# Shared tiles for the last keys of a cross-attention, and a key bias that rides as one more column

## The chip, the cores and the metric

The kernel runs on one core of one Trainium2 chip. The time is the device time of one execution in microseconds (us). Three executions of the kernel before took 1998.29, 2001.81 and 2000.94 us; their median is 2000.94. One more execution was profiled.

The engines are named as in the profile: PE (TensorE's matmuls), PEld (its weight loads), DVE (VectorE), ACT (ScalarE), POOL (GpSimd), SP (the queue that issues the DMAs).

## The reference, cut to what matters

Eight batches of 64 tokens go through one block of three parts: cross-attention over a context of 1601 tokens together with a self-attention, a sparse attention, and a feed-forward network with ternary weights. The change touches the cross-attention:

```python
# x: (8, 64, 512), cond = ctx_2048: (8, 1601, 512); 16 heads of 128, 8 groups of keys
qx = _fp8_linear_pertensor(ln_out, wqx, wqx_scale, qx_in_scale).reshape(b, s, g, hpg, d)
qx = _ln(qx, qxln_w, qxln_b)
kvx = jnp.einsum('bsi,oi->bso', cond, w_kv_x)
kx, vx = jnp.split(kvx, 2, axis=-1)
kx = _ln(kx.reshape(b, sc, g, d), kxln_w, kxln_b)      # weight and bias per key element
vx = vx.reshape(b, sc, g, d)
xout = _gqa(qx, kx, vx).reshape(b, s, nh * d)          # softmax(q k / sqrt(128)) v
```

A key is a normalised vector times `kxln_w` plus `kxln_b`. The bias adds the same number to all scores of one query row.

## The kernel before, in words

The 8 groups of keys are worked in two halves of 4 (`HG = 4`). One `Cross(b, half)` object does one batch for one half; there are 16 of them, half 0 first, batches 0 to 7 in each. The 1601 context tokens are cut into 13 tiles of 128 (`TT`); the last has 65 (1601 = 12 x 128 + 65). Six chunks of two tiles, the last of three (128 + 128 + 65 = 321), share a tile of keys and one of scores.

A hand-written loop over `g` (16 x 13 steps and a run-out of 20, 228 in all) sets the order of tracing. In step `g` it calls, each for another tile:

- `keys(tt)`: load a transposed context tile `cTr`, split it into a rounded high part (`cThi`, ACT) and the rest (`cTlo`, POOL), and form the key products on PE: three combinations of high and low parts by four pieces of the 512 inputs, twelve matmuls of 512 columns (L542). Then square and copy on ACT (L547, L548), sum on DVE (L549), the inverse root on POOL (L550, L173), and the scaling on DVE (L552). The mean is already taken out of the weights.
- `keys_t(tt)`, one step later: four transposes on PE (L219), then the scaled and biased key as high part `kthi` (ACT, L565), the scaled rest `kf` (DVE, L567), and the low part `ktlo`, which is `kf` plus the bias (ACT, L568).
- `scores(ci)` when a chunk is whole: three matmuls for each group (L587) and one DVE pass that moves the scores from PSUM and takes their row maximum (L591). The odd width 321 is filled up to 322 by zeroed key columns (POOL).
- `maxima`, `exps`, `probs_t`, `context`, `weigh` and `values`, some 13 to 17 steps later (`LAG = 17`): exponentials (L601), turned probabilities (L613), and their product with the context tile (L673 to L678), which is loaded again as `cr`.

All other work is written as generators in three streams, pumped at the end of every step: `bgA` (projections, self-attention and the tail of every token block) at `PACE[0]` yields a step until `g = LATER`, then `PACE[1]`; `bgB` (ternary weights) and `bgC` (the last token blocks). At step 135 the loop empties `bgA` in one go, before the batch halves of half 1 are concatenated.

A scheduler then draws up a fixed order for each engine: it takes what is ready in its own timeline, by priority, which is the order of tracing unless the code shifts it. `issue_after(pin[0].ins)` keeps background work on DVE behind the scaling of the newest keys. PSUM has 8 banks: 3 (`pm`) are shared by scores, keys, turned probabilities and values once the first steps are over, 1 is for the background, 4 hold the context sums.

Of the kernel before, what the change touches and what calls it, by code (L numbers as in the profile page):

```python
# [11 lines left out]
F32 = mybir.dt.float32  # L12
# [24 lines left out]
KTW = 324  # L37
NCH = len(CHUNKS)
CHUNK_OF = {tt: ci for ci, ch in enumerate(CHUNKS) for tt in ch}
LAG = 17  # L40
# [4 lines left out]
FAR = 3  # L45
PACE = 1.55, 4
LATER = 142
TERNARY_PACE, TERNARY_AT = 0.4, 8
# [9 lines left out]
def tile_perceiver(ctx: ExitStack, tc: tile.TileContext, t: dict):  # L58
# [432 lines left out]
    def key_weights(half):  # L491
# [11 lines left out]
        return hi, lo  # L503

    paced = [None]
    pin = [None]

    class Cross:


        def __init__(self, b, half):
            self.b, self.half = b, half
            self.raw = None
            self.S = {}
            self.kt = {}
            self.kn = {}
            self.pp = {}
            self.cc = {}
            self.mx = sm("cmx", HG * NCH, bufs=2)
            self.su = sm("csu", HG * NCH, bufs=2)  # L520

# [7 lines left out]
        def keys(self, tt):  # L529

            t0, n = TT[tt]
            raw = mp.tile([P, NIC, P], F32, tag="raw", name=nm("cTr"), bufs=3)
            paced[0] = nc.sync.dma_start(raw[:, :, :n], t["ctxT"][self.b].rearrange("(c p) k -> p c k", p=P)[:, :, t0:t0 + n])
            chi = mp.tile([P, NIC, P], F32R, tag="cThi", name=nm("cThi"), bufs=2)
            clo = mp.tile([P, NIC, P], F32R, tag="cTlo", name=nm("cTlo"), bufs=2)
            A.copy(chi[:, :, :n], raw[:, :, :n])  # L536
            GP.tensor_tensor(clo[:, :, :n], raw[:, :, :n], chi[:, :, :n].bitcast(F32), ALU.subtract)  # L537
            ps = kxp()
            k = 0
            for st, mv in ((chi, self.wk[0]), (chi, self.wk[1]), (clo, self.wk[0])):  # L540
                for ic in range(NIC):
                    PE.matmul(ps[:n], lhsT=st[:, ic, :n], rhs=mv[:, ic, :], start=k == 0, stop=k == 11)  # L542
                    k += 1
            kn = mp.tile([P, 512], F32, tag="kn", name=nm("kn"), bufs=3)
            sq = mp.tile([P, 512], F32, tag="sq", name=nm("sq"), bufs=1)
            v = sm("kxv", HG)
            A.activation(sq[:n], ps[:n], AF.Square, scale=1.0 / math.sqrt(D))  # L547
            A.copy(kn[:n], ps[:n])  # L548
            V.tensor_reduce(v[:n], v3(sq[:n], HG), AX.X, ALU.add)  # L549
            GP.tensor_scalar(v[:n], v[:n], EPS, None, ALU.add)  # L550
            r = rsqrt(v[:n], n, HG, "rqk")
            pin[0] = V.tensor_tensor(v3(kn[:n], HG), v3(kn[:n], HG), r.unsqueeze(2).to_broadcast([n, HG, D]), ALU.mult)  # L552
            self.kn[tt] = kn

        def keys_t(self, tt):

            t0, n = TT[tt]
            ci = CHUNK_OF[tt]
            c0 = TT[CHUNKS[ci][0]][0]
            if ci not in self.kt:  # L560
                self.kt[ci] = [mp.tile([P, HG, KTW], F32R, tag="kt" + x, name=nm("kt" + x), bufs=2) for x in ("hi", "lo")]
            hi, lo = self.kt[ci]
            pt = transpose4(self.kn.pop(tt), n, kxp())
            o = slice(t0 - c0, t0 - c0 + n)
            A.activation(hi[:, :, o], v3(pt, HG)[:, :, :n], AF.Identity, bias=hb["kx"], scale=hw["kx"])  # L565
            kf = mp.tile([P, HG, P], F32, tag="kf", name=nm("kf"), bufs=2)
            V.scalar_tensor_tensor(kf[:, :, :n], v3(pt, HG)[:, :, :n], hw["kx"], hi[:, :, o].bitcast(F32), ALU.mult, ALU.subtract)  # L567
            A.activation(lo[:, :, o], kf[:, :, :n], AF.Identity, bias=hb["kx"])  # L568

        def scores(self, ci):  # L570
# [3 lines left out]
            N = cw + (cw & 1)  # L574
            if N > cw:
                GP.memset(hi[:, :, cw:N].bitcast(F32), 0.0)
                GP.memset(lo[:, :, cw:N].bitcast(F32), 0.0)
            sc = mp.tile([P, HG, KTW], F32, tag="S", name=nm("S"), bufs=7)
            self.S[ci] = sc
            per = 512 // N  # L580
            for g0 in range(0, HG, per):
# [7 lines left out]
                for i, g in enumerate(gs):  # L589
                    ps = bank[:, i * N:(i + 1) * N]  # L590
                    V.tensor_tensor_reduce(sc[:, g, :cw], ps[:, :cw], zeros.to_broadcast([P, cw]), 1.0, -3.0e38,  # L591
                                           ALU.add, ALU.max, self.mx[:, g * NCH + ci:g * NCH + ci + 1])

        def maxima(self):
            self.nmx = sm("cnm", HG)
            V.tensor_reduce(self.nmx, v3(self.mx, HG), AX.X, ALU.max, negate=True)  # L596

# [371 lines left out]

    def gp_copy(dst, src):  # L970
        GP.tensor_scalar(dst, src, 1.0, 1.0, ALU.mult, ALU.mult)  # L971

    WIDEN = gp_copy, A.copy
# [155 lines left out]

    NT = len(TT)  # L1130
    work = [Cross(b, half) for half in range(2) for b in range(NB)]
# [10 lines left out]
    for g in range(NA + LAG + 3):  # L1142
# [27 lines left out]
        if g == 0:  # L1170
            bgA.pump(ALL)
        if g == 2:
            bgA.add(norms(rest), projection("qx", range(4), rest), projection("qx", range(4, 8), range(NJ)),
# [51 lines left out]
        for bg, q in ((bgA, PACE[g >= LATER]), (bgC, PACE[1]), (bgB, TERNARY_PACE if g < NA + FFN_AT else 0)):  # L1225
            n = int((g + 1) * q) - int(g * q)

            with tc.issue_after(pin[0].ins), tc.issue_after(paced[0].ins) if bg is bgB else nullcontext():
                bg.pump(n)
# [79 lines left out]
```

## Time and profile before

| | |
|---|---|
| median of three executions | 2000.94 us |
| the profiled execution | 1998.47 us |
| its span, first to last instruction | 1996.7 us |
| mean granted PE clock | 0.987 |
| PE matmuls | 10709, busy 1931.5 us |
| L542, twelve key products for each of 208 tiles | 832 + 832 + 832 matmuls |
| L568, low part of the keys on ACT | 208, busy 147.4 us |
| DMA, hardware queue | 349.97 MB, 55.8% of 16 engines |

In a row of grouped instructions the first number after the bar is the busy time of the group and the second the mean duration of one in ns; matmuls overlap, so durations of PE add up to more than the time they take. In a timeline row stand start, length, engine, line, what is written from what, shapes and a count. In a row of waits stand the total in us, how often, and the longest.

### The profile page before, as it was taken

What the parts mean: (1) busy time and instruction counts of PE and PEld (TensorE: products, weight loads), DVE (VectorE), ACT (ScalarE), POOL (GpSimd) and SP (SyncE); (2) the same over time, 40 slices, a digit from 0 to 9 for tenths busy, and PEclk for the clock granted to TensorE, in tenths of its full rate; (3) what the DMA queues carried; (4) which work ended last, traced back from release to release, by engine and by line L of the source; (5) the groups of instructions that cost most, each with busy time, mean ns of one, the idle gap of its engine ahead of it and who ended that gap; (6) DMA issues with size and microseconds to landing.
All of it is one profiled execution on the core that took longest, in us unless ns stands there. A gap on an engine that the chain in (4) does not pass through costs nothing. (4 is left out here: it accounts for less than half of the span.)

```text
span 1996.7 us, 32526 instructions
## 1 busy us (share of the span) xinstructions
PE 1931.5 (97%) x10709; PEld 1594.1 (80%) x10709; DVE 1357.9 (68%) x3324; ACT 1345.9 (67%) x2932; POOL 682.7 (34%) x807
## 2 busy tenths in 40 slices
PE   6899999999999999999999999999999999999998
PEld 5688887888888888888888888888877777886776
DVE  6868678667778677766775765666577665665665
ACT  6777777677778667765765655665786676676554
POOL 5443434333334434323233323323333323320132
PEclk9999999999999999999999999999999999999989
DMA  6354445466455654556886667656744633564415
GB/s 195 112 151 148 148 146 153 132 193 213 152 150 172 194 179 140 173 180 224 282 268 192 214 225 264 203 185 214 258 133 154 212 110 97 165 205 139 149 56 172
DMA packets 296507, 352.05 MB, mean 176 GB/s; under 512 B 30337, under 2 KB 191233, under 8 KB 296337
## 3 DMA queue, kind: packets, MB, share of 16 engines
q1 hardware_dynamic: 296336, 349.97, 55.8%
q8 instruction: 84, 1.38, 0.3%
q14 instruction: 87, 0.70, 0.1%
HBM read 283.94 MB, written 65.68 MB: 175 GB/s over the span
## 5 line engine op out<-in xcount | busy, mean ns | idle before, releaser
L537 POOL TENSOR_TENSOR cTlo<-cTr,cThi 128x512 fp32r<-128x512 f32 (+1 forms) x208 | 271.1, 1303 | 840.7 <-PE kx L542 443.8
L677 PE MATMUL acc<-plo,chi 128*128 128x512 f32 x768 | 311.7, 406 | 1.0 <-DVE plo L624 1.0
L678 PE MATMUL acc<-phi,clo 128*128 128x512 f32 x768 | 303.4, 396 | 0.0
L549 DVE TENSOR_REDUCE kxv<-sq 128x4 f32<-128x512 f32 (+1 forms) x208 | 141.9, 682 | 228.0 <-ACT sq L547 227.7
L542 PE MATMUL kx<-wkhi,cThi 128*128 128x512 f32 (+1 forms) x832 | 244.3, 415 | 6.6 <-DVE cmx L591 2.5
L676 PE MATMUL acc<-phi,chi 128*128 128x512 f32 x768 | 237.8, 403 | 4.6 <-ACT chi L653 3.4
L565 ACT ACTIVATE kthi<-kx,cols 128x512 fp32r<-128x512 f32 (+1 forms) x208 | 159.5, 767 | 106.8 <-PE kx L219 105.1
L542 PE MATMUL kx<-wklo,cThi 128*128 128x512 f32 (+1 forms) x832 | 231.0, 398 | 0.0
L542 PE MATMUL kx<-wkhi,cTlo 128*128 128x512 f32 (+1 forms) x832 | 226.3, 393 | 0.0
L173 POOL TENSOR_TENSOR rqk<-kxv,mhalf 128x4 f32<-128x4 f32 (+1 forms) x208 | 219.9, 1057 | 16.6
L653 ACT CAST chi<-cr 128x512 fp32r<-128x512 f32 x192 | 118.9, 619 | 137.7 <-PE acc L677 126.2
L536 ACT CAST cThi<-cTr 128x512 fp32r<-128x512 f32 (+1 forms) x208 | 125.6, 605 | 120.0 <-PE kx L542 48.4
L601 ACT ACTIVATE S<-S,cnm 128x256 f32<-128x256 f32 (+1 forms) x384 | 196.8, 520 | 1.5 <-DVE cnm L596 1.5
L567 DVE SCALAR_TENSOR_TENSOR kf<-kx,cols,kthi 128x512 f32<-128x512 f32 (+1 forms) x208 | 151.1, 726 | 60.0 <-ACT kthi L565 58.8
L542 PEld LDWEIGHTS kx<-wklo,cThi 128*128 128x128 f32 (+1 forms) x832 | 156.2, 188 | 39.7
L542 PEld LDWEIGHTS kx<-wkhi,cTlo 128*128 128x128 f32 (+1 forms) x832 | 153.5, 185 | 39.3 <-issue 0.8
L552 DVE TENSOR_TENSOR kn<-kn,rqk 128x512 f32<-128x512 f32 (+1 forms) x208 | 144.7, 695 | 57.0 <-POOL rqk L173 55.5
L542 PEld LDWEIGHTS kx<-wkhi,cThi 128*128 128x128 f32 (+1 forms) x832 | 147.2, 189 | 40.8 <-DVE cmx L591 5.0
L591 DVE CUSTOM_DVE_ANT_0 S<-s,zeros 128x256 f32<-128x256 f32 (+1 forms) x384 | 149.7, 429 | 43.8 <-PE s L587 43.5
L568 ACT ACTIVATE ktlo<-kf,cols 128x512 fp32r<-128x512 f32 (+1 forms) x208 | 147.4, 709 | 29.0 <-DVE kf L567 28.5
L676 PEld LDWEIGHTS acc<-phi,chi 128*128 128x128 f32 x768 | 139.0, 189 | 34.9 <-ACT chi L653 4.6
L677 PEld LDWEIGHTS acc<-plo,chi 128*128 128x128 f32 x768 | 145.2, 189 | 25.7 <-DVE plo L624 1.5
(339 smaller groups left out, 3938.3 us busy)
## 6 DMA issues: line engine op xcount, KB each, us to landing
cTr<-in_ctxT SPq DMA_DIRECT2D x192, 256.0 KB
cr<-in_ctx SPq DMA_DIRECT2D x192, 256.0 KB
ws<-wpd SPq DMA_DIRECT2D x88, 512.0 KB
clod<-clo SPq DMA_DIRECT2D x96, 256.0 KB
clo<-clod SPq DMA_DIRECT2D x96, 256.0 KB
wv<-in_wkv SPq DMA_DIRECT2D x64, 256.0 KB
tern<-in_ffn_w SPq DMA_DIRECT2D x64, 256.0 KB
wpd<-ws SPq DMA_DIRECT2D x32, 512.0 KB
```

The source lines that it names most:

```text
L173: GP.tensor_tensor(y[:n], v, mhalf[:n, :k], ALU.pow)
L537: GP.tensor_tensor(clo[:, :, :n], raw[:, :, :n], chi[:, :, :n].bitcast(F32), ALU.subtract)
L542: PE.matmul(ps[:n], lhsT=st[:, ic, :n], rhs=mv[:, ic, :], start=k == 0, stop=k == 11)
L552: pin[0] = V.tensor_tensor(v3(kn[:n], HG), v3(kn[:n], HG), r.unsqueeze(2).to_broadcast([n, HG, D]), ALU.mult)
L565: A.activation(hi[:, :, o], v3(pt, HG)[:, :, :n], AF.Identity, bias=hb["kx"], scale=hw["kx"])
L567: V.scalar_tensor_tensor(kf[:, :, :n], v3(pt, HG)[:, :, :n], hw["kx"], hi[:, :, o].bitcast(F32), ALU.mult, ALU.subtract)
L568: A.activation(lo[:, :, o], kf[:, :, :n], AF.Identity, bias=hb["kx"])
L591: V.tensor_tensor_reduce(sc[:, g, :cw], ps[:, :cw], zeros.to_broadcast([P, cw]), 1.0, -3.0e38, ALU.add, ALU.max, self.mx[:, g * NCH + ci:g ...
L601: A.activation(self.S[ci][:, g, :cw], self.S[ci][:, g, :cw], AF.Exp, bias=self.nmx[:, g:g + 1], accum_out=self.su[:, g * NCH + ci:g * NCH ...
L676: PE.matmul(self.U[ic], lhsT=chi[:n, s], rhs=phi[:n], start=tt == 0, stop=False)
L677: PE.matmul(self.U[ic], lhsT=chi[:n, s], rhs=plo[:n], start=False, stop=False)
L678: PE.matmul(self.U[ic], lhsT=clo[:n, s], rhs=phi[:n], start=False, stop=False)
```

## The change

Four things change.

1. **The 64 tokens before the odd one.** Tile 12 (tokens 1536 to 1599) of batches 2k and 2k+1 is loaded into one tile of 128 rows when the even batch comes to it, and one set of twelve products gives the keys of both. The odd batch's `keys(12)` returns at once; its rows wait in the tile `kn2` until its own `keys_t(12)`. The first two batches of half 0 are left unpaired (`UNPAIRED = 2`) and keep their tile of 65.
2. **The odd token.** `odd_keys` forms, once for each half (at `g = 30` and `g = 110`), the keys of token 1600 of all eight batches in one tile of eight rows. Each paired batch copies its column from there into its chunk (ACT).
3. **The keys' bias.** Keys are only scaled now: high part by ACT (`turned`), low part by DVE straight into `ktlo`. The bias becomes a key of its own, in the column that was zero before (column 322 of the last chunk). Its score, one number for each query row, is copied out of PSUM for each group (`qb`), and `maxima` adds it to the largest score and forms `qb - (top + qb)` as the exponent's offset.
4. **Order and memory.** `PACE` goes from 1.55 to 1.57, `LATER` from 142 to 145, pumped background work is traced under `tc.high_priority(-100)`, so 100 places later in priority, and the scratch for software DMA descriptors shrinks to 1024 bytes of a partition.

```diff
+NT = len(TT)
+ODD_AT = 30, 110
+UNPAIRED = 2
-PACE = 1.55, 4
-LATER = 142
+PACE = 1.57, 4
+LATER = 145
...
+    def turned(kn, n, parts, r0=0):
+        hi, lo = parts
+        pt = kxp()
+        for g in range(HG):
+            PE.transpose(pt[:, g * P:g * P + n], kn[:, g * P:(g + 1) * P], ident[r0:r0 + n, r0:r0 + n])
+        src = v3(pt, HG)[:, :, :n]
+        A.activation(hi, src, AF.Copy, scale=hw["kx"])
+        V.scalar_tensor_tensor(lo, src, hw["kx"], hi.bitcast(F32), ALU.mult, ALU.subtract)
+
+    def odd_keys(half):
+        raw = load(mp.tile([P, 512], F32, tag="raw", name=nm("oc"), bufs=3)[:NB], t["ctx"][:, SC - 1, :])
+        pt = kxp()
+        for ic in range(NIC):
+            PE.transpose(pt[:, ic * NB:(ic + 1) * NB], raw[:, ic * P:(ic + 1) * P], ident[:NB, :NB])
...
+        A.copy(chi[:, :, :NB], src)
+        V.tensor_tensor(clo[:, :, :NB], src, chi[:, :, :NB].bitcast(F32), ALU.subtract)
+        kn = normed_keys(wk[half], chi, clo, NB)
+        oddk[half] = [const.tile([P, HG, NB, 2], F32R, tag=f"odd{x}", name=nm("odd")) for x in ("h", "l")]
+        for x, y in zip(oddk[half], kb2):
+            gp_copy(x[:, :, :, 1], y.bitcast(F32).unsqueeze(2).to_broadcast([P, HG, NB]))
+        turned(kn[:NB], NB, [x[:, :, :, 0] for x in oddk[half]])
...
+    V.tensor_copy(kb, hb["kx"].to_broadcast([P, HG]))
+    V.tensor_copy(kb2[0], kb)
+    V.tensor_tensor(kb2[1], kb, kb2[0].bitcast(F32), ALU.subtract)
...
         def keys(self, tt):
             t0, n = TT[tt]
+            pair = tt == NT - 1 and self.paired
+            if pair and self.b % 2:
+                return
...
+            if pair:
+                n = P
+            for bi in range(2 if pair else 1):
+                w = S if pair else n
+                paced[0] = nc.sync.dma_start(raw[:, :, bi * S:bi * S + w], t["ctxT"][self.b + bi].rearrange("(c p) k -> p c k", p=P)[:, :, t0:t0 + w])
...
+            self.kn[tt] = normed_keys(self.wk, chi, clo, n, pair)
+            if pair:
+                work[self.half * NB + self.b + 1].kn[tt] = self.kn[tt]
...
         def keys_t(self, tt):
-            pt = transpose4(self.kn.pop(tt), n, kxp())
-            o = slice(t0 - c0, t0 - c0 + n)
-            A.activation(hi[:, :, o], v3(pt, HG)[:, :, :n], AF.Identity, bias=hb["kx"], scale=hw["kx"])
-            kf = mp.tile([P, HG, P], F32, tag="kf", name=nm("kf"), bufs=2)
-            V.scalar_tensor_tensor(kf[:, :, :n], v3(pt, HG)[:, :, :n], hw["kx"], hi[:, :, o].bitcast(F32), ALU.mult, ALU.subtract)
-            A.activation(lo[:, :, o], kf[:, :, :n], AF.Identity, bias=hb["kx"])
+            o = t0 - c0
+            kn = self.kn.pop(tt)
+            if tt < NT - 1 or not self.paired:
+                turned(kn[:n], n, [x[:, :, o:o + n] for x in self.kt[ci]])
+                if n & 1:
+                    for x, y in zip(self.kt[ci], kb2):
+                        gp_copy(x[:, :, o + n:o + n + 1], y.bitcast(F32).unsqueeze(2))
+                return
+            r = self.b % 2 * S
+            turned(kn[r:r + S], S, [x[:, :, o:o + S] for x in self.kt[ci]], r)
+            for x, y in zip(self.kt[ci], oddk[self.half]):
+                A.copy(x[:, :, o + S:o + S + 2], y[:, :, self.b, :])
...
         def scores(self, ci):
-            if N > cw:
-                GP.memset(hi[:, :, cw:N].bitcast(F32), 0.0)
-                GP.memset(lo[:, :, cw:N].bitcast(F32), 0.0)
...
+                    if N > cw:
+                        V.tensor_copy(self.qb[:, g:g + 1], ps[:, cw:N])
 
         def maxima(self):
+            top = sm("ctop", HG)
+            V.tensor_reduce(top, v3(self.mx, HG), AX.X, ALU.max)
+            V.tensor_tensor(top, top, self.qb, ALU.add)
             self.nmx = sm("cnm", HG)
-            V.tensor_reduce(self.nmx, v3(self.mx, HG), AX.X, ALU.max, negate=True)
+            V.tensor_tensor(self.nmx, self.qb, top, ALU.subtract)
...
+        if g in ODD_AT:
+            odd_keys(work[nA].half)
...
-            with tc.issue_after(pin[0].ins), tc.issue_after(paced[0].ins) if bg is bgB else nullcontext():
+            with tc.issue_after(pin[0].ins), tc.issue_after(paced[0].ins) if bg is bgB else nullcontext(), tc.high_priority( -100):
                 bg.pump(n)
...
-    nc = _bacc.Bacc("TRN2", target_bir_lowering=False, num_devices=1)
+    nc = _bacc.Bacc("TRN2", target_bir_lowering=False, num_devices=1, dynamic_dma_scratch_size=1024)
```

`normed_keys` is the second part of the old `keys` (products, squares, norm and scaling) as a function of its own; for a paired tile it writes to `kn2`, of which there is one, instead of `kn`, of which there are three.

## The prediction

> **What bounds the kernel now.** I read the page's first two parts, then the waits of TensorE (PE), then a timeline of single tiles, since busy time does not give the price of one matmul.
>
> ```profile
> span 1996.7 us, 32526 instructions
> PE 1931.5 (97%) x10709; PEld 1594.1 (80%) x10709; DVE 1357.9 (68%) x3324; ACT 1345.9 (67%) x2932; POOL 682.7 (34%) x807
> PE   6899999999999999999999999999999999999998
> PEclk9999999999999999999999999999999999999989
> ```
>
> PE is busy in every slice but the first two and the last; no other engine passes 68%, and the granted clock is full. So 1996.7 - 1931.5 = 65 us of the span are PE idle. The waits of PE say where, longest first:
>
> ```profile
> PE tr L219 <- DVE fa L201: 11.7, 2, 10.6
> PE pj L340 <- ACT ws L325: 5.0, 1, 5.0
> ...
> PE pt L613 <- DVE cmx L591: 3.9, 5, 1.4
> ...
> PE acc L676 <- ACT chi L653: 3.4, 2, 2.8
> PE kx L219 <- DVE kn L552: 3.0, 2, 1.9
> PE tr L372 <- ACT fb L385: 2.9, 1, 2.9
> PE pt L613 <- ACT S L601: 2.8, 2, 2.6
> PE kx L542 <- DVE cmx L591: 2.5, 6, 0.6
> PE pp L431 <- DMA ws<-wpd: 2.5, 3, 1.3
> ```
>
> The columns are total us, times, longest. Nothing repeats in every tile: 208 key tiles and 208 context tiles go by with some dozens of waits. Between the start and the last 150 us the kernel lasts as long as PE's instructions do. What one tile costs is read from starts, not from durations (here PE's timeline around one full tile, one 65-token tile, and the transposes of a 65-token tile):
>
> ```profile
> 707.95 1.09 PE L542 MATMUL kx<-wkhi,cThi 128*128 128x512 f32 x4
> 708.88 1.07 PE L542 MATMUL kx<-wklo,cThi 128*128 128x512 f32 x4
> 709.78 1.07 PE L542 MATMUL kx<-wkhi,cTlo 128*128 128x512 f32 x4
> ...
> 758.02 1.18 PE L542 MATMUL kx<-wkhi,cThi 128*65 128x512 f32 x4
> 759.03 1.10 PE L542 MATMUL kx<-wklo,cThi 128*65 128x512 f32 x4
> 759.97 1.10 PE L542 MATMUL kx<-wkhi,cTlo 128*65 128x512 f32 x4
> 760.91 0.60 PE L219 MATMUL kx<-ident,kn 128*128 128x128 f32 x4
> ...
> 768.69 0.41 PE L219 MATMUL kx<-ident,kn 65*128 65x65 f32 x4
> 768.93 0.61 PE L613 MATMUL pt<-ident,S 128*128 128x128 f32 x4
> ```
>
> A 65-token tile's twelve products run from 758.02 to 760.91, 2.89 us; a full one's first eight from 707.95 to 709.78, 1.83 us, so 2.75 for twelve. Sixty-five tokens cost what 128 cost. I use 2.8 us a tile, 0.234 a matmul. A small transpose is (768.93 - 768.69)/4 = 0.06 us.
>
> **The change part by part, TensorE.** Pairing starts at batch 2 in half 0 and at batch 0 in half 1: 3 + 4 = 7 pairs, so 7 of 208 key tiles disappear: 7 x 2.8 = 19.6 us less. The transposes stay, four a tile and batch (64 columns for 65). `odd_keys` runs twice; its eight tokens still move 512 columns in each of twelve products: 2 x 2.8 = 5.6 us more, and 16 small transposes at 0.06 are 1.0. The scores keep their 322 columns: the last, once zero, now holds the bias key. PE's work: -19.6 + 5.6 + 1.0 = **-13.0 us**.
>
> Two other prices were possible. By the page's mean (406 to 415 ns a matmul) 84 fewer and 24 more would be worth 60 x 0.41 = 25 us. Durations overlap: four of 0.4 us start within 0.93. And the Trainium skill ("TensorE: Matmul & The Clock Gate", section "Back-to-back issue gap") puts a sustained 512-column matmul in a real kernel at about 131 ns; by that the removed tiles save 11.0 us, the added cost 3.1, and PE gains only 7 us. The starts above say 0.225 to 0.24, so the measured number decides and I keep 13.0.
>
> **ScalarE (ACT).** The low part of the keys is now the subtraction itself, so L568 goes: 208 x 0.709 = 147 us. Five fewer tiles net (7 gone, 2 small come) take 5 x (0.59 + 0.58) = 6 of squares and copies. The odd columns add 28 copies at about 0.2 (nearest row: the 128x4 copy L633, 199 ns median), 5.6 us. ACT ends near 1346 - 147 = 1199 us, perhaps 19 less if the high part without bias is 0.09 shorter (L346, a scaled copy of 128x512 from PSUM, is 687 ns; L565 782). ACT is not the bound, so only PE waits that end in ACT can shrink. The rows above plus smaller ones make about 17 us, 2.2 of them the first weights, untouched. Gain between 0 and 13; with a tenth of ACT's work gone I take a third of 13: **-4 us**. What is late next in those waits is PE's own earlier work or DVE.
>
> **VectorE (DVE).** L567 writes the low part instead of `kf`, at the same 0.73. New in the last chunk are 4 copies of one PSUM column for each of 16 batch-halves: 64. No row of that shape; nearest is L817, a 64x8 copy from PSUM, 164 ns median: 10.5 us of DVE, covered on DVE itself at 68%. But each holds a score bank that long; before, a bank was held for 486 + 83 ns. PE now loses 3.9 + 2.5 = 6.4 us to L591. Bounds: 0 if another bank is free, 10.5 if every copy shows. A hold longer by 164/569, 29%, of waits of 6.4 gives **+2 us**. The two additional operations in `maxima` (about 0.17 each, as L596) delay the first exponentials by 0.35 us; probabilities are turned two loop steps later, some 17 us, which hides them; without that cover, 16 x 0.35 = 5.6. Three operations for `kb` at the start: at most 0.6, I take 0.3 into rounding.
>
> **GpSimd and the queues.** POOL loses 32 memsets of 0.103 and 5 x 1.3 of norms; it gains 4 + 4 small copies near 0.26. It is 34% busy: nothing. SP issues the same 208 key loads (each pair's tile takes two) plus two small ones, 0.38 us each, and the loads queued behind them are prefetched. `odd_keys` has a chain (load, transpose, copy, product, norm, transpose). PE's order is fixed at build, so a link that comes late holds everything behind it on PE. Bounds: 0, and 2 x 3 us by the longest PE waits on ACT and DVE in the middle (2.6 to 2.9): **+2 us**. `kn2` lives 13 loop steps, and the next pair wants it after 26; it holds nobody. In the odd batch's empty step PE moves 2.8 us earlier to the next tile, whose load may show; PE has no wait at all on `cTr` now, and ACT waits 16.0 us in total for it, so nothing taken.
>
> **Order and pace.** Background work (projections, self-attention, the tail of each token block) gets 100 places less priority; a loop step has 32526/228, about 143, instructions, so it yields by two thirds of a step. PE now waits on background tiles (pj, tr of L372, pp) 5.0 + 2.9 + 2.5 = 10.4 us; yielding gives their producers more time. No row prices a reordering: bounds -10 and +10 (it can create as many such waits), I take a fifth of what is to be had, **-2 us**. Pace 1.57 brings 3 steps ahead by loop step 135, where all the remaining background is issued at once (I count about 227 steps in all, so some 18 remain instead of 21). Between there and step 148 that queue is empty, so moving the switch from 142 to 145 changes nothing. The smaller scratch moves no data in this kernel: the page shows the hardware queue and instruction queues only. Nothing.
>
> Sum: -13.0 - 4 + 2 + 2 - 2 = **-15 us**. The profiled execution took 1998.47 (its span and 1.8 around it), so 1983.5 there. That execution lies 2.5 under the median of the runs, 2000.94; on the median the forecast is **1986 us**.
>
> **The rivals.**
> - More than the sum. ACT's relief and the new order remove half of the 65 us of idle PE time that is not start or tail (about 30 us): -13 - 15 = -28 or so, 1972. For it: many waits end in ACT or on background tiles. Against: some are PSUM banks waiting for DVE, which is not relieved. Chance 0.15.
> - Background deferred too far (the slower one). Its place is the producers of background tiles: weight splits on ACT and DVE (L325, L327), norms through POOL (44 `rq` powers of about 1.07 us). Placed behind the foreground, they end after PE's fixed order has arrived at their consumer. Price: one such wait for each of 227 background steps. It decides from 15/227 = 0.066 us a step; at 0.13 it costs 30, net +15, 2016. For it: the one 5.0 us wait of pj on ws shows how a late split hits PE. Against: only a handful of such waits now, with DVE and ACT a third idle. Chance 0.14, weighed at 2003 to 2020.
> - Banks. Every one of 64 column copies delays PE by its time and a signal, 0.25 us: 16 us instead of 2, net -1, 2000. Against: L591 shows in 11 PE waits while 384 banks pass. Chance 0.04.
> - PE's work falls but something else sets the pace, so nothing is seen: 1999 to 2002. Against: 97%. Chance 0.05.
>
> **How the numbers follow.** Main case 0.62, own range 1977 to 1996. Differences under 0.2%, 4 us, can hardly be told from none here: the three runs of before span 1998.29 to 2001.81. Faster by more than that: 0.62 + 0.15 = 0.77. Same: banks and nothing, 0.04 + 0.05, less a little given to slower: 0.08. Slower: 0.15. The range takes the main case, most of the larger gain and the no-change cases, with one tenth below and one above: 1968 to 2003.
>
> **What would show it.** PE's busy time near 1912 to 1920 with about 10665 matmuls, and L542's successor with 12 x 203 of them; ACT near 1180 to 1200 with no `ktlo` row on ACT; PE's idle between 58 and 66 us. The waits on `cmx` should be near 8 us, no more than 15. Wrong if PE's busy time falls by 13 and idle rises as much (the order), if new rows of pj, tr or pp waiting stand at the top of PE's waits, or if a transpose of `odd_keys` waits many us. A fall of the idle below 45 us is the larger gain.

## The result, and the profile after

The changed kernel took 2008.07 us (median of 8 executions, 2003.40 to 2014.02) beside 2001.01 us of the kernel before (8 executions, 1995.88 to 2003.34). The ratio is 1.0040, interval 1.0025 to 1.0055: slower by about 7 us, where 1986 us was forecast and 2003 was the upper end of the range. Each run below had the kernel before beside it on its chip, with medians of 1999.55 to 2001.45 us; two runs are best compared by their ratios to it.

From the page of the profile after, the span and the busy times:

```profile
span 2003.2 us, 32385 instructions
PE 1924.9 (96%) x10665; PEld 1593.9 (80%) x10665; DVE 1376.2 (69%) x3417; ACT 1206.4 (60%) x2739; POOL 673.6 (34%) x766
```

PE has 44 matmuls fewer and is busy 6.6 us less; ACT lost 139.5 us. But PE's idle is now 2003.2 - 1924.9 = 78.3 us, against 65.2 before. The work went down as meant, and the idle time rose by twice as much. The waits of PE (total us, times, longest) show where part of it shows up:

```profile
PE tr L222 <- DVE fa L204: 11.8, 3, 10.1
PE tr L375 <- ACT fa L370: 5.6, 4, 2.7
PE pj L343 <- ACT ws L328: 5.0, 1, 5.0
...
PE pt L676 <- DVE cqb L651: 4.0, 1, 4.0
...
PE po L488 <- ACT fb L480: 2.8, 1, 2.8
```

The two longest of before are still there, nearly unchanged (11.7 and 5.0 us). One row is new near the top, the `tr` transposes of background work that wait for `fa` of ACT (5.6 us in four waits). The bank waits have not grown in sum: those on `cmx`, 6.4 us before, are 1.9 in all, and the new copies `cqb` add 4.0 in a single wait. No one row carries what the change costs. So I used another reading. For every matmul I take the time to the next one's start. The median of that for its shape, over all the traces here (capped at 0.231 us for 512 columns), is its *work*; whatever a matmul takes beyond it is *stall*, which holds waits and slow clock alike. Before: work 1857.5, stall 124.7 us. After: work 1847.7, stall 141.5. The change saves 9.8 us of work and brings 16.8 us of stall.

One place shows how such a stall comes about: the odd keys of half 1, in PE's timeline (start, length, line, what, shapes, count; in brackets the idle time before):

```profile
964.79 0.41 PE L544 MATMUL kx<-ident,oc 8*128 8x8 f32 x4
...
967.08 1.08 PE L514 MATMUL kx<-wkhi,cThi 128*8 128x512 f32 x4
967.99 1.07 PE L514 MATMUL kx<-wklo,cThi 128*8 128x512 f32 x4
968.90 1.07 PE L514 MATMUL kx<-wkhi,cTlo 128*8 128x512 f32 x4
971.26 0.63 PE L222 MATMUL tr<-ident,fa 128*128 128x128 f32 x4 [1.29 <-DVE fa L476]
974.66 2.07 PE L488 MATMUL po<-fb,ld 64*128 64x128 f32 x8 [2.78 <-ACT fb L480]
976.66 1.63 PE L532 MATMUL kx<-ident,kn 8*128 8x8 f32 x8
978.09 1.06 PE L676 MATMUL pt<-ident,S 128*128 128x128 f32 x4
...
981.08 2.07 PE L514 MATMUL kx<-wkhi,cThi 128*128 128x512 f32 x4
982.96 1.73 PE L514 MATMUL kx<-wklo,cThi 128*128 128x512 f32 x4
```

Between the end of the odd products and their transposes at 976.66 PE has only twelve background matmuls (L222, L488), and these wait too. By the last two rows four products take 1.88 us, from 981.08 to 982.96, twice the 0.91 of the odd products above. The table by stretches (busy time and count of PE, PEld, DVE, ACT, POOL; then the granted clock, DMA share, GB/s) says why:

```profile
965.00:970.00 5.00, 4.97 (x24) 2.58 (x22) 3.73 (x7) 2.48 (x5) 1.39 (x2) 1.00 0.78 200
970.00:974.00 4.00, 0.63 (x4) 0.42 (x4) 1.34 (x4) 1.44 (x3) 0.75 (x1) 1.00 1.04 349
974.00:978.00 4.00, 3.34 (x16) 3.09 (x17) 2.24 (x6) 0.90 (x3) 1.73 (x3) 0.51 0.69 253
978.00:982.00 4.00, 4.00 (x16) 3.35 (x15) 2.94 (x7) 2.67 (x7) 0.00 (x0) 0.50 0.00 0
```

PE is idle 3.4 of 4 us from 970, and for the next ten its clock is halved. PE looks 100% busy in the last row: half of that is loss which no wait shows.

What PE waited for stands on ACT in the same stretch, from the timeline of all engines:

```profile
972.56 0.62 ACT L604 CAST cThi<-cTr 128x512 fp32r<-128x512 f32 x1 [3.19 <-DMA cTr<-in_ctxT]
973.08 0.58 ACT L519 ACTIVATE sq<-kx 8x512 f32<-8x512 f32 x1
973.57 0.56 ACT L520 COPY kn<-kx 8x512 f32<-8x512 f32 x1
974.04 0.57 ACT L480 COPY fb<-tr 128x512 f32<-128x512 f32 x1
974.79 1.02 POOL L176 TENSOR_TENSOR rqk<-kxv,mhalf 8x4 f32<-8x4 f32 x1
975.85 0.68 DVE L524 TENSOR_TENSOR kn<-kn,rqk 8x512 f32<-8x512 f32 x1 [1.48 <-POOL rqk L176]
```

ACT's order is fixed as well. It waits 3.19 us for a context load, with the squares of the odd keys and the copy `fb` queued behind. From square to scaled key the chain takes another 3.5 us, and the transposes stand behind it in PE's order.

### The profile page after: what moved, and what is told of

It reads as the page before. It is cut to its first block, busy times and chain, and to the rows that moved or that the text cites. A ratio compares the mean times of both kernels' runs of the same rounds, so it can differ in the third digit from the quotient of the medians.

```text
span 2003.2 us, 32385 instructions
## 1 busy us (share of the span) xinstructions
PE 1924.9 (96%) x10665; PEld 1593.9 (80%) x10665; DVE 1376.2 (69%) x3417; ACT 1206.4 (60%) x2739; POOL 673.6 (34%) x766
## 4 chain that ended last, share of the span: by engine, by line
PE 79%; DVE 7%; DMA 6%; ACT 3%; issue 2%; POOL 2%; SPq 0%; POOLq 0%; ACTq 0%; DVEq 0%
PE kx L514 24%; PE acc L739 8%; PE acc L740 7%; PE acc L741 7%; PE s L644 6%; PE pt L676 4%; PE pj L343 4%; PE kx L532 4%; PE xo L760 3%; DMA cTr<-in_ctxT 3%; PE pp L434 2%; PE p L868 1%; PE po L488 1%; PE y L1119 1%; DMA ws<-wpd 1%
## 5 line engine op out<-in xcount | busy, mean ns | idle before, releaser
L514 PE MATMUL kx<-wkhi,cThi 128*128 128x512 f32 x812 | 236.3, 412 | 6.1 <-ACT wkhi L504 2.3
L514 PE MATMUL kx<-wklo,cThi 128*128 128x512 f32 x812 | 226.5, 399 | 0.0
L514 PE MATMUL kx<-wkhi,cTlo 128*128 128x512 f32 x812 | 225.0, 395 | 0.0
L534 ACT ACTIVATE kthi<-kx,cols 128x512 fp32r<-128x512 f32 (+2 forms) x208 | 140.6, 676 | 114.8 <-PE kx L532 113.4
L535 DVE SCALAR_TENSOR_TENSOR ktlo<-kx,cols,kthi 128x512 fp32r<-128x512 f32 (+2 forms) x208 | 150.6, 724 | 63.8 <-ACT kthi L534 62.6
L514 PEld LDWEIGHTS kx<-wklo,cThi 128*128 128x128 f32 x812 | 154.9, 191 | 38.7 <-issue 1.6
L514 PEld LDWEIGHTS kx<-wkhi,cTlo 128*128 128x128 f32 x812 | 152.8, 189 | 35.6 <-issue 0.8
L514 PEld LDWEIGHTS kx<-wkhi,cThi 128*128 128x128 f32 x812 | 146.0, 191 | 39.1 <-ACT wkhi L504 3.5
L519 ACT ACTIVATE sq<-kx 128x512 f32<-128x512 f32 (+1 forms) x203 | 121.6, 599 | 73.9 <-PE kx L514 70.3
L741 PEld LDWEIGHTS acc<-phi,clo 128*128 128x128 f32 x768 | 144.8, 189 | 24.8 <-issue 0.8
```

Of the source, the lines that this page charges most:

```text
L534: A.activation(hi, src, AF.Copy, scale=hw["kx"])
L535: V.scalar_tensor_tensor(lo, src, hw["kx"], hi.bitcast(F32), ALU.mult, ALU.subtract)
L741: PE.matmul(self.U[ic], lhsT=clo[:n, s], rhs=phi[:n], start=False, stop=False)
```

## The experiments

All runs in one table, in us; "work" and "stall" are read from each kernel's one profiled execution as above. That execution lies up to 5.7 us from its kernel's median (old_pace: 2012.69 beside 2018.35), so differences of stall below some 6 us say little.

| kernel | time | ratio to before | interval | work | stall |
|---|---|---|---|---|---|
| changed kernel | 2008.07 | 1.0040 | 1.0025-1.0055 | 1847.7 | 141.5 |
| no_priority | 2023.85 | 1.0116 | 1.0103-1.0129 | 1847.7 | 158.9 |
| old_pace | 2018.35 | 1.0091 | 1.0077-1.0105 | 1847.7 | 149.1 |
| data_only | 2016.69 | 1.0083 | 1.0068-1.0098 | 1847.7 | 155.5 |
| order_only | 1991.17 | 0.9957 | 0.9944-0.9970 | 1857.5 | 117.7 |
| pace_only | 2001.89 | 1.0007 | 0.9994-1.0021 | 1857.5 | 128.7 |
| bias_only | 2002.29 | 1.0010 | 1.0000-1.0021 | 1857.5 | 125.7 |
| pair_only | 2016.10 | 1.0087 | 1.0063-1.0112 | 1847.7 | 154.2 |
| bias_dropped | 1994.98 | 0.9974 | 0.9964-0.9985 | 1857.5 | 121.7 |
| pairs_in_half_1 | 2005.72 | 1.0028 | 1.0017-1.0039 | 1851.5 | 137.2 |
| odd_private | 2019.74 | 1.0097 | 1.0076-1.0119 | 1847.7 | 156.5 |
| odd_left_out | 1996.75 | 0.9990 | 0.9975-1.0004 | 1840.9 | 143.3 |
| odd_left_out_new_pace | 2015.71 | 1.0080 | 1.0058-1.0102 | 1840.9 | 157.9 |
| pair_repeated | 2033.29 | 1.0166 | 1.0134-1.0198 | 1867.1 | 150.1 |
| odd_spread | 2004.84 | 1.0027 | 1.0014-1.0039 | 1847.7 | 135.9 |
| changed_odd_spread | 2006.08 | 1.0041 | 1.0025-1.0057 | 1847.7 | 143.2 |
| combined | 1994.78 | 0.9966 | 0.9952-0.9979 | 1851.5 | 126.1 |
| order_no_bias | 1993.62 | 0.9975 | 0.9966-0.9984 | 1857.5 | 119.9 |
| all_spread | 1994.09 | 0.9980 | 0.9969-0.9991 | 1847.7 | 130.3 |

### Is it the order or the data?

**no_priority**, **old_pace** and **data_only** keep all of the data change and undo the order's two edits, one at a time and together; **order_only** is the kernel before with the priority alone.

```diff
 no_priority
-..., tc.high_priority( -100):
+...:
 old_pace
-PACE = 1.57, 4
-LATER = 145
+PACE = 1.55, 4
+LATER = 142
 order_only (on the kernel before)
-with tc.issue_after(pin[0].ins), ...:
+with tc.issue_after(pin[0].ins), ..., tc.high_priority(-100):
```

> The changed kernel with one part undone: background work keeps its place in priority (no shift by 100 places). Theory O (the new order is the loss: background behind the foreground reaches PE late, which cost about 20 us of stalls against 12 us of saved PE work): 1985 to 1992, ratio to before 0.992 to 0.996, PE idle back near 65 us. Theory P (the pairing itself is the loss: an odd batch's empty step brings PE to loads and banks that are not ready): still 2003 to 2010, ratio 1.001 to 1.005.

> The changed kernel with pace 1.55 and the switch at step 142 as before; all else as changed. Both theories, O and P, say that pace does not matter: 2003 to 2012. A third, R (any small change of order redraws the fixed schedule and moves the time by 5 to 10 us either way), allows 1995 to 2018; a result under 2000 would speak for R.

> Pairing, odd keys and bias column with the old order: pace 1.55, switch at 142, no shift in priority. O: 1985 to 1992 like the first kernel here. P: 2003 to 2012. R: anywhere from 1985 to 2012 and more than 5 us away from the first.

> The kernel before with one thing added: background work 100 places later in priority; no pairing, no bias column. O: 2015 to 2025 (20 us of stalls and no saved work), ratio 1.007 to 1.012. P: 1996 to 2003. R: within 10 us of before on either side.

The lower priority is no loss: alone it gains 0.43%, 8.4 us; its stall is 10.0 us lower in the first four batches and 3 higher in the rest. The loss is in the data, 0.83% with the old order. The first three kernels came out slower than any theory had put them. But the two edits of the order do not add. With the data changed, the lower priority alone brings +1.7 us (2016.69 to 2018.35), the pace alone +7.2 (to 2023.85), and both together -8.6 (to 2008.07). PE's matmuls are the same in the four kernels.

### Which part of the data change?

**bias_only** has the bias column and no pairs, **pair_only** the pairs and the odd keys with the bias added as before, and **bias_dropped** leaves out the bias and its column (old order in all three; the smaller scratch stays, so it is in the +2 us of bias_only too and is not the loss).

```diff
 bias_only
-self.paired = half > 0 or b >= UNPAIRED
+self.paired = False
 pair_only (in turned)
-A.activation(hi, src, AF.Copy, scale=hw["kx"])
-V.scalar_tensor_tensor(lo, src, hw["kx"], ...)
+A.activation(hi, src, AF.Identity, bias=hb["kx"], scale=hw["kx"])
+V.scalar_tensor_tensor(kf, src, hw["kx"], ...)
+A.activation(lo, kf, AF.Identity, bias=hb["kx"])
 bias_dropped (read against the kernel before)
-A.activation(lo[:, :, o], kf[:, :, :n], AF.Identity, bias=hb["kx"])
...
```

> The bias column alone, with the order of before: keys are only scaled, the bias is a key in column 322, no tile is shared and no odd token is taken out. Theory P (sharing tiles in half 0 costs more than it saves): 1990 to 2002, PE idle 60 to 68 us. Theory B (the bias column is the loss: its copies hold score banks and lengthen the way from the last chunk to the exponentials): 2012 to 2022, with the stalls in the steps after a batch's last chunk. PE's work is that of before in both.

> Shared tiles and odd keys alone, with the order of before; the bias is added to the keys by ACT as before (L568 is back) and the spare column is zero. P: 2008 to 2022, PE work 12 us down and stalls 30 us up. B: 1984 to 1992.

> As the bias-only kernel, but with the bias left out altogether: it adds one number to all scores of a row, which the softmax takes out again. No column copies, the spare column is zero, the maxima are one operation. It has the shorter way to the keys and nothing of the column. P: within 4 us of the bias-only kernel. B: 1985 to 1997 and at least 15 us faster than the bias-only kernel.

The column is worth nothing either way (+2 us). Pairing carries the loss: 0.87% alone, with stall 29.5 us above before and work 9.8 below. bias_dropped gains 5 us, which fits a relief of ACT that the column takes back; a mere redraw of the order can be as large (below), so that reading is not shown. The rows of the changed kernel, by shape (busy, mean ns):

```profile
L534 ACT ACTIVATE kthi<-kx,cols 128x512 fp32r<-128x512 f32 x192 | 132.8, 692 | 112.7 <-PE kx L532 111.4
L651 DVE COPY cqb<-s 128x1 f32<-128x1 f32 x64 | 9.7, 151 | 0.0
L657 DVE TENSOR_TENSOR ctop<-ctop,cqb 128x4 f32<-128x4 f32 x16 | 7.2, 449 | 0.3
```

The key's high part takes 692 ns instead of 782, a column copy 151; these were sized rightly.

### Where do the pairs lose?

> All of the data change, but tiles are shared in half 1 only (4 pairs, one set of odd keys), with the order of before. P: half 1 has little background work, so the saved 4 x 2.8 - 3.3 = 8 us show there: 1985 to 1996, 20 us or more faster than with pairs in both halves. B: 2008 to 2022, since every batch keeps the column.

```diff
 pairs_in_half_1 (on data_only)
-ODD_AT = 30, 110
-UNPAIRED = 2
+ODD_AT = 110,
+UNPAIRED = 8
```

With 2005.72 us it missed the range. I cut the traces into batches, each from its first key product to that of the next. Against bias_only, the batch in which the odd keys are formed (batch 0 of half 1) became 15.0 us longer, of which 5.2 were work and 9.8 stall. The rest of half 1, with the tail, became 8.9 us shorter: 11.3 us less work (11.2 expected from 4 x 2.8) and 2.4 more stall. In these two executions the pairs pay, and the place of the odd keys does not.

Three theories for that place were told apart. **odd_private** gives the odd keys' tiles memory of their own instead of the pools shared with foreground keys. **odd_left_out** leaves out the odd keys' computation (their column is filled with the bias key). **pair_repeated** has the odd batch load and multiply the pair's tile again, so that no loop step of PE is empty; its keys then lie in `kn`, not in `kn2`.

```diff
 odd_private
-raw = load(mp.tile([P, 512], F32, tag="raw", name=nm("oc"), bufs=3)[:NB], ...)
+raw = load(const.tile([P, 512], F32, tag="oc", name=nm("oc"))[:NB], ...)
-chi = mp.tile([P, NIC, P], F32R, tag="cThi", ...)
+chi = const.tile([P, NIC, NB], F32R, tag="ochi", ...)
...
 odd_left_out
-raw = load(...)
-...
-kn = normed_keys(wk[half], chi, clo, NB)
...
 pair_repeated
-if pair and self.b % 2:
-    return
```

> The data change with the order of before (2017 us with shared buffers), but the odd keys work in buffers of their own: the loaded rows, their high and low parts and the normed keys no longer take one of the three context buffers, the two split buffers and the three key buffers. Theory H (the odd rows held a context buffer for some 25 us, so context loads behind them came late): 1996 to 2006, stalls about 20 us fewer and no gap of 14 us between two cTr loads around the odd keys. Theory E (the empty step of the odd batch is the loss): 2012 to 2020.

> The same kernel without the chain of the odd keys: the odd token's key is left out and its column filled with the bias key. It bounds what the chain costs: 6.6 us of PE work for both halves and its stalls. H: 1990 to 2000, a little below the kernel with private buffers. E: 2006 to 2014, only the 6.6 us of work and a few more.

> The data change with the order of before, but the odd batch loads the pair's tile and forms its products once more instead of taking them from the even batch: no empty step, and 7 x 2.8 = 20 us of PE work back. H: the saved work is lost and the odd chain still stalls: 2028 to 2042. E: 2005 to 2018, since the stalls of the empty step go with it.

Memory is not it: 2019.74 us, 3 us above data_only. The empty step is not it: filling it costs 16.6 us, hardly less than the 19.4 us of added work. Leaving the chain out gains 19.9 us against data_only, where it saves 6.8 us of work. So in the old order the chain costs some 13 us beyond its work.

### The chain, undone as a chain

In odd_private PE's timeline around the odd products of half 1 reads:

```profile
966.94 1.09 PE L514 MATMUL kx<-wkhi,oclo 128*8 128x512 f32 x4
968.65 0.51 PE L434 MATMUL pp<-ws,cats 128*128 128x512 f32 x1 [0.63 <-ACT ws L424]
969.38 1.11 PE L434 MATMUL pp<-ws,cats 128*128 128x512 f32 x3 [0.22 <-DVE ws L425]
973.45 3.65 PE L466 MATMUL sc<-ld,qT 128*128 128x64 f32 x16 [2.97 <-DMA ld<-kd]
977.03 1.64 PE L532 MATMUL kx<-ident,kn 8*128 8x8 f32 x8
```

Behind the products stand the odd transposes, and only background that is not ready was drawn in between. This made the theory that the loss lies in tracing the whole chain in one loop step, where every other key tile has a step between products and transposes. **odd_spread** is odd_private with a pause after the split and another after the products' norm, so that the three parts are traced in three steps; **changed_odd_spread** does the same to the changed kernel.

```diff
+        yield
         kn = normed_keys(wk[half], chi, clo, NB, "kn3")
+        yield
...
-        if g in ODD_AT:
-            odd_keys(work[nA].half)
+        if g in ODD_AT:
+            oddgen[0] = odd_keys(work[nA].half)
+        if g - 2 in ODD_AT or g - 1 in ODD_AT or g in ODD_AT:
+            next(oddgen[0])
```

> The data change with the order of before and private buffers for the odd keys (2020 us), with one thing more: their chain is traced over three loop steps instead of one (transposes at step g, products at g + 1, the turning of the normed keys at g + 2), as the other tiles are. Theory C (PE stands in its fixed order before the odd keys' last transposes until ACT, DVE and POOL have normed them, some 5 us each time, and its clock halves after): 1998 to 2008, near the kernel without the chain (1997) plus 7 us of work. If something else of the chain costs (its work on ACT, DVE, POOL, or the PSUM banks): 2012 to 2022.

> The changed kernel itself (pace 1.57, background 100 places later) with private buffers and the chain of the odd keys spread over three steps. C: 2008 - 12 to 20 = 1988 to 1998. Otherwise 2003 to 2012.

With the old order the theory held: 2019.74 to 2004.84 us, -14.9, and stall falls by 20.6, 10 of them in batch 0 of half 1. The same stretch of odd_spread, PE's timeline and the table of stretches:

```profile
968.93 0.85 PE L514 MATMUL kx<-wkhi,oclo 128*8 128x512 f32 x3
...
979.95 0.41 PE L532 MATMUL kx<-ident,kn 8*128 8x8 f32 x4
```

```profile
965.00:975.00 10.00, 10.00 (x54) 7.26 (x53) 6.75 (x17) 5.70 (x13) 3.77 (x5) 1.00 0.84 291
975.00:985.00 10.00, 10.00 (x64) 8.49 (x63) 7.25 (x13) 6.96 (x17) 2.17 (x3) 1.00 0.66 208
```

Ten us of other work now lie between the last product and the first transpose, and the clock stays full. The groups of PE by shape say it in one row each, first data_only, then odd_spread (the first number after the second bar is PE's idle time before the group):

```profile
L532 PE MATMUL kx<-ident,kn 8*128 8x8 f32 x8 | 0.8, 208 | 4.7 <-DVE kn L524 4.7
```

```profile
L532 PE MATMUL kx<-ident,kn 8*128 8x8 f32 x8 | 0.8, 207 | 0.0
```

On the changed kernel the same edit gave nothing: its ratio to before is 1.0041 beside 1.0040, and the expectation of 1988 to 1998 was missed. Where did the gain go? The chain falls into batch 2 of half 0 and batch 0 of half 1. This is the stall of these two batches in all twenty traces, in us:

| | batch 2 of half 0 | batch 0 of half 1 |
|---|---|---|
| chain in one step (7 kernels; 9 in half 1) | 4.9 to 10.3 | 11.1 to 18.9 |
| chain spread or left out (5) | 0.5 to 4.4 | 6.8 to 11.3 |
| no odd keys in that half (8; 6 in half 1) | 0.0 to 3.3 | 3.8 to 9.2 |
| before | 3.3 | 7.9 |
| changed kernel | 6.6 | 17.8 |
| changed_odd_spread | 4.4 | 7.3 |

So a chain in one step costs its own two batches stall in every order tried: on average 4.5 and 7 us more than where it is spread or left out (the ranges touch in half 1, 11.1 beside 11.3). From the kernel before to the changed one they account for 13.2 of the 16.8 us. Spreading the chain takes 12.7 us away from them in the changed kernel as well, but there the other batches rise by 14.4 us together (6.3 in batch 6 of half 1, 5.7 in batch 7 of half 0, smaller ones elsewhere), while under the old order they fell by 6.6. The local cost is shown; that undoing it brings the time back holds in one order and not in the other.

### What remains: the schedule itself

With the chain left out the pairs should give 16.6 us of work; odd_left_out gained 5.5 against bias_only. Do the remaining 11 us belong to the pairs, or to the schedule that was drawn? **pace_only** changes the pace on the kernel before, **odd_left_out_new_pace** on odd_left_out (1.57 and 145 for 1.55 and 142 in both, as the changed kernel has it).

> The kernel before with one edit: pace 1.57 in place of 1.55 and LATER 145 in place of 142. Theory R (any edit of the order redraws the fixed schedule by several us, without a cost of its own): the time moves by 3 to 10 us, in either direction. The rival, that the pace has an effect of its own and small: the order alone gained 9 to 10 us on the kernel before, and on the changed kernel the pace was worth 10 us of gain, so the pace alone would gain up to 10 us here too, 1990 to 2000. A time of 2003 to 2010 would say that the sign of the pace's effect depends on the rest of the schedule.

> odd_left_out (pairs in both halves, bias as a column, old order, the odd keys' chain left out and its column filled with the bias key) with pace 1.57 and LATER 145. odd_left_out took 1996.75 us, some 11 us more than the saved products predict. Theory R: this remainder is a matter of the schedule drawn, so the time moves by 3 to 10 us with the pace, in either direction. The rival, a stall that belongs to the paired tiles as such: the time stays within 3 us of 1996.75, since the number of paired tiles is the same.

The kernel before does not care: +0.4 us. The paired kernel does: +19 us (18 by the ratios), with the same matmuls, and in the profiled executions, 14.4 us apart in span, all of it is stall (143.3 to 157.9). It also bounds what leaving out the chain is worth. With the new pace and the old priority the chain's kernel is no_priority, 2023.85 us: there the same cut gives 8.1 us (7.2 by the ratios), little more than its 6.8 us of work, where it gave 19.9 with the old pace. There too the chain's two batches lose 13 us of stall, and the others take 12. Theory R, a redraw of the fixed order without a cost of its own, is right for the paired kernel, by more than expected, and missed for the kernel before. One candidate for how: ACT waits for context loads. The waits of ACT on them, in the kernel before and in the changed one:

```profile
ACT cThi L536 <- DMA cTr<-in_ctxT: 16.0, 16, 3.0
```

```profile
ACT cThi L604 <- DMA cTr<-in_ctxT: 71.0, 37, 5.0
```

Loads are late more often with the change, and each late one holds what stands behind it on ACT. But the sum does not follow the time: 73.4 and 71.2 us in odd_left_out and odd_left_out_new_pace, which are 19 us apart, and 71.9 us in all_spread, which is faster than before. So it can hurt at one place, as shown at 972.56, and is not the explanation of the rest. That rest stays open.

### Versions meant to beat both

**combined** takes the lower priority, pairs in half 1 only, private odd tiles and no bias; **order_no_bias** is the kernel before with the lower priority and the bias left out; **all_spread** has the pairs in both halves, the spread chain, the lower priority, the old pace and no bias.

```diff
 combined: order_only + bias_dropped + pairs_in_half_1 + odd_private
 order_no_bias: order_only + bias_dropped
 all_spread: odd_spread + order_only + bias_dropped
```

> Put together: tiles shared in half 1 only, odd keys in private buffers, the bias left out (the softmax removes it), background 100 places later, pace 1.55. If the parts add up: 2000 - 8 (order) - 5 (bias left out) - 13 + 4 (pairs and odd keys) = 1978; if the odd keys stall with private buffers too, 1985 to 1992. If a schedule with several changes loses what each gained, 1995 or more.

> No shared tiles and no odd keys: the kernel before with the bias left out and background 100 places later, pace 1.55. If the two gains add up: 2000 - 8 - 5 = 1987. If each only redraws the schedule: 1990 to 2000.

> Shared tiles in both halves, private odd keys spread over three steps, bias left out, background 100 places later, pace 1.55. If the saved PE work (13 us) now shows on top of the kernel without shared tiles: 1974 to 1980. If shared tiles stall in half 0 for another reason too: 1985 to 1998.

They gain 5.6 to 6.2 us, none as much as the priority alone, though the intervals overlap. Had the parts added up, 1978, 1987 and 1974 to 1980 us were expected. Gains measured one by one, -8.4 and -5.1 us, give -6.2 together in order_no_bias. With the chain spread the pairs save 9.8 us of work in all_spread and cost 10.4 us of stall against order_no_bias. The fastest kernel measured, and the one I would keep, is order_only: 1991.17 us, 0.9957 (0.9944 to 0.9970).

## Why the prediction was wrong, point by point

**The failed step** is the sentence on `odd_keys`: "Bounds: 0, and 2 x 3 us by the longest PE waits on ACT and DVE in the middle (2.6 to 2.9): +2 us". For the +2 us, the stall of the two batches that hold the chain rose by 13.2 us; in the old order the chain cost 13 us (odd_left_out) to 15 us (odd_spread) beyond its work. The sentence named the mechanism, a late link holds everything behind it on PE. It was mis-sized by taking the longest wait of a kernel in which every chain was spread over loop steps. The chain's own length was in the rows: square, sum, two steps on POOL and the scaling, 0.60 + 0.68 + 0.26 + 1.05 + 0.70, some 3.3 us without hand-overs, twice. And the price of a slower clock after the wait was not in the sum at all: 5.1 of the 13.2 us, at the odd keys of half 1, as the last section shows.

**The sum as such** failed too. It adds local prices to a total, and the total did not follow them: in changed_odd_spread the chain's 12.7 us are gone from its batches, and the time stayed. Stall was forecast at -2 us in all (-4 + 2 + 2 - 2) and came to +16.8. The chain's batches hold 13.2 of that; no term accounts for the rest, nor for what rises elsewhere when the chain is mended. A redrawn order alone moved the same matmuls by up to 19 us; how it does so stays open.

**The order** was costed at a fixed -2 us within +-10. Alone, on the kernel before, it is -8.4. On the changed data it is +1.7 with the old pace and -15.8 with the new one. "No row prices a reordering" was right; that it has no fixed price either was missing. The same holds for the pace, costed at nothing: +0.4, +7.2, -10.3 and +19.0 us by what else is in the kernel. The 2 x 2 of order and pace on the same matmuls spreads over 15.8 us, as much as the whole forecast gain. The range had no place for it.

**PE's work**, -13.0 us, measured -9.8. Seven pairs saved 19.4 (84 matmuls at 0.231) for 19.6 forecast, the odd products cost 5.5 for 5.6, and the small transposes 1.3 for 1.0. Missing were 2.8 us in "The transposes stay, four a tile and batch": among matmuls of 128 rows, 64 rows are dearer than 65, as the last section shows.

**The start-to-start reading** held. The key products alone save 13.9 us by their measured steps (19.4 - 5.5), and 14.0 had been forecast. The durations make it 25 us, and 131 ns a matmul, the sustained figure of the Trainium skill ("TensorE: Matmul & The Clock Gate", section "Back-to-back issue gap"), makes it 7.9. That the prediction's 7 us by that figure, transposes included, lies as near the 9.8 as its 13.0 is chance: the transposes it sized wrongly fill the gap.

**ACT**, -4 us: the relief is there (1206 us busy, forecast near 1199). Without the column 5 us were gained, which may be it. With the column, bias_only gains nothing. So ACT and the banks together, forecast at -2, came to +2; the interval of bias_only reaches from 0 to +4.

**The empty step** of the odd batch, "nothing taken", is not refuted: filled again, in pair_repeated, the time rose by 16.6 us for 19.4 us of work, and that difference is within the intervals.

**The rivals.** "Background deferred too far" forecast a loss by the order; order_only refutes it for the kernel before. "Banks" asked 16 us of the column; bias_only and bias_dropped, with and without it, are 7 us apart, and no bank wait of that size stands in the rows. Of the profile's signs, "PE's busy time falls by 13 and idle rises as much (the order)" came true in its second half, idle +13 with busy -6.6, but its cause was not the order alone. "A transpose of `odd_keys` waits many us" looked at the right place. It shows in data_only (4.7 us), not in the changed kernel, where background matmuls stand before these transposes and wait in their stead:

```profile
L532 PE MATMUL kx<-ident,kn 8*128 8x8 f32 x8 | 1.0, 230 | 0.0
```

## What to carry to other kernels

Work that is rare and small is not cheap where an engine's order is fixed: price a new chain by the length of its hand-overs, and by whether work that is ready was placed between its links, not by its instructions. Trace it over several steps, as its neighbours are, and then measure the total again: a local cost that is gone need not leave the total. Before you credit an edit with under 1% on a scheduler-drawn kernel, run it in a second order (another pace, another priority): here the same matmuls moved by 16 to 19 us.

## What the runs showed of the hardware

**A stall is paid nearly twice.** In the changed kernel PE did 0.63 us of work from 970.7 to 974.1 and then ran at half clock to about 984.3; the same in the kernel before at 350:

```profile
970.70:974.10 3.40, 0.63 (x4) 0.42 (x4) 0.81 (x2) 1.54 (x4) 0.85 (x1) 1.00 1.05 357
974.10:977.50 3.40, 2.84 (x14) 2.59 (x15) 1.64 (x4) 0.72 (x3) 1.63 (x3) 0.50 0.77 286
977.50:980.90 3.40, 3.40 (x16) 3.03 (x14) 2.63 (x7) 2.65 (x8) 0.00 (x0) 0.50 0.00 0
980.90:984.30 3.40, 3.40 (x10) 2.54 (x9) 2.38 (x5) 0.10 (x2) 0.00 (x0) 0.50 0.60 193
984.40:987.70 3.30, 3.30 (x22) 2.91 (x21) 1.42 (x6) 1.70 (x3) 1.85 (x3) 1.00 0.29 111
```

```profile
346.70:350.10 3.40, 1.42 (x10) 0.95 (x9) 3.40 (x17) 2.78 (x7) 0.00 (x0) 1.00 0.56 169
350.10:353.50 3.40, 3.40 (x9) 2.61 (x9) 2.97 (x8) 1.55 (x5) 0.35 (x1) 0.50 0.34 108
353.60:356.90 3.30, 3.30 (x23) 2.96 (x22) 1.08 (x3) 2.92 (x7) 2.67 (x4) 1.00 0.12 40
```

In the changed kernel 10.2 us at 0.50 are 5.1 us lost, behind some 4 us of idle (1.29 + 2.78). The length differs: 3.4 us in the kernel before at 350, 6.8 in data_only from 977.3 to 984.1. The Trainium skill ("TensorE: Matmul & The Clock Gate", section "What's actually happening") has the halving after at least one idle window of about 3.4 us and the full clock back after at least one busy one. The lengths, one, two and three times 3.4 us, agree with the second. By the first no halving was due and the 5.1 us were not lost: the 3.4 us before each halving were not idle, PE was busy for 0.63, 0.80 (data_only) and 1.42 us of them. The measurement decides.

Over the whole kernel this is little. Mean granted clocks of 0.987 and 0.986 over spans of 1996.7 and 2003.2 us make 26 us lost before and 28 after, so some 2 of the 16.8 us of stall.

**Among matmuls of 128 rows, 64 rows cost more than 65.** Four transposes of 65 rows and what follows, in PE's timeline of the kernel before, and two groups of four with 64 rows in the changed kernel:

```profile
1122.47 0.41 PE L219 MATMUL kx<-ident,kn 65*128 65x65 f32 x4
1122.72 0.61 PE L613 MATMUL pt<-ident,S 128*128 128x128 f32 x4
```

```profile
1145.49 0.46 PE L532 MATMUL kx<-ident,kn 64*128 64x64 f32 x4
1145.88 0.66 PE L676 MATMUL pt<-ident,S 128*128 128x128 f32 x4
```

```profile
1035.18 1.16 PE L488 MATMUL po<-fb,ld 64*128 64x128 f32 x8
1036.18 0.40 PE L532 MATMUL kx<-ident,kn 64*128 64x64 f32 x4
1036.51 0.66 PE L676 MATMUL pt<-ident,S 128*128 128x128 f32 x4
```

The next work starts after 0.25 us with 65 rows and after 0.39 at 1145.49. Within such a group the starts are 112, 62, 62 and 153 ns apart with 64 rows, and 59 to 64 with 65. The matmul ahead pays too: one of 128 rows and 512 columns takes 320 ns to the start of a matmul of 64 rows, and 230 to one of 65 (medians over all traces, without idle time between). It is the change of rows that costs, not the 64 rows: the group at 1036.18 follows matmuls of 64 rows, its first step is 56 ns and the step before it 111. Some 90 ns before a group and 145 in it make an estimate of 3.3 us for the 14 paired groups. Why the change costs is not shown by these runs.
